# Gathers of a conv-attention kernel taken image by image, and a quarter of the third image's keys and values made inside the attention

## The chip, the cores and the metric

The kernel runs on one core of a Trainium2 chip. The metric is the device time of one execution in microseconds (us). The core has five engines that work side by side, each through its own list of instructions: PE (TensorE, matmuls and transposes), DVE (VectorE), ACT (ScalarE), POOL (GpSimd) and SP (SyncE, which here only issues DMAs). They meet at semaphores.

## The reference

The input `x` is four images of 32 x 32 positions with 384 channels, in float32. Layer 0 is a deformable attention: queries, a grouped 3 x 3 convolution that gives each query and group a sampling offset, bilinear sampling of the input there, keys and values from the samples, and an attention of 1024 queries by 1024 keys for each of 4 x 6 = 24 image-and-head units, with a position bias that is itself sampled bilinearly. Cut to what matters:

```
q = gn(x) @ w_q
o = gelu(layernorm(grouped_conv3x3(q)))
pos = tanh(o @ w_offp) * 16 + ref            # for each query and each of 6 groups
xs = bilinear_sample(gn(x), pos)
k, v = xs @ w_k, xs @ w_v
attn = softmax(q_h . k_h * scale + bilinear_sample(rpe, (ref - pos) / 2))
x = x + (attn @ v) @ w_out
```

Layer 1, a linear attention and a mixture of four experts on the result, follows. The change doesn't touch it.

## The kernel before, in words

**Stage A** makes, for all four images, what the attention needs. An image b is split into two halves f of 512 positions, and into eight blocks k of 128. The steps have one-letter names in the code:

- x and rec load an image (`x`) and write the records that are gathered later (`img`); T transposes it; S is the group norm's statistics.
- Q makes queries, C the convolution (L712, with its copies L724 and L738 on ACT), N the offsets: statistics (L761), scaling (L774 on ACT, L778 and L780 on DVE), Gelu (L782), products and sums (L788, L795), Tanh (L799), then nine small DVE operations from `pos` (L802) to the gather's indices `pidx` (L823), and after them the weights of the four corners and `widx`, the indices of the attention's windows. N comes in halves of an image; image 0's first half comes in two quarters.
- G is `fetch(b, k)` (L866): six indirect DMAs by POOL (L870), one for each group, into one of four buffers `ga`. M is `sampled(b, k)` (L880): three DVE operations (L885, L889, L890) that weight and sum the corners into `xs`.
- X transposes a sampled half (L256, copied with scale and shift by ACT, L262), K makes its keys (three blocks, `keys_of`, L269; ACT L278; stored by SP, L281), V its values (four blocks, `values_of`, L285; ACT L294; stored by SP, L298). `mm` and `tr` are the PSUM buffers that they take.

The order of these steps is not left to a scheduler at run time. `Plan.emit` (L118) simulates the stage: each step has an engine, a cost, a rank and needs, and some take and give back buffers; the step that can start first goes first, by rank where several can. The ranks are shifted by the table `SHIFT`, with an entry for each group of steps. The outcome is a fixed order of instructions on PE, ACT, DVE, POOL and SP, written out by hand. In the program's final order the attention's first window gather (POOL) and its `upper` (ACT) stand ahead of the last steps of stage A.

Image 3 is different: its samples are made in stage A, but its X, K and V are left to the attention (`if b == B - 1: continue`).

**Stage B, the attention**, runs 24 units i in six heads for each image, in four steps kp each, so 96 steps g. A step holds two blocks of 128 keys by 1024 queries. POOL gathers two windows of the bias (`fetch_windows`, L1161), which are interpolated by ACT (`upper`, L1177), DVE (`lower`, L1187) and ACT (`left`, L1195). PE adds scores and bias in PSUM (L1214, L1219) and DVE finishes them (`right`, L1245), runs the maximum (L1263), subtracts (L1304); ACT takes the exponential (L1308), PE multiplies with the values (L1322) and sums (L1331), ACT copies the result (L1347). A one-column copy on ACT, the `token` (`turn_over`, L1234), tells PE that a score buffer is free. Five steps of the loop overlap: step g runs scores of g + 1, `upper` of g + 2 and values of g - 5.

Between these, `late` is a list of pieces: for each half of image 3, two transposes, three keys and four values. `last_image(0)` puts one piece on PE in a PSUM tile `pl` at the end of an even step, unless the output projection (`project`) has blocks waiting; `last_image(1)` evacuates it by ACT and stores it by SP in the next odd step. So pieces are made at kp 0 or 2. Step 60 loads weights for what follows (`load_early`).

**Stages C and D**, layer 1, follow from about 1750 us.

Of the kernel before, what the change touches and what calls it, by code (L numbers as in the profile page):

```python
# [20 lines left out]
B, HI, WI, NC = 4, 32, 32, 384  # L21
N = HI * WI
NB = N // P
CK = NC // P
G, GC = 6, 64
# [24 lines left out]


SHIFT = {
    ("ACT", "N", 0, 2): 71.86, ("ACT", "N", 3, 4): -5.4, ("ACT", "S", 2): -1.66,
    ("ACT", "evac", 0): 9.11, ("ACT", "evac", 3): -1.37, ("DVE", "M", 0, 0): 25.81,
    ("DVE", "M", 1, 0): 43.51, ("DVE", "N", 0, 0): 2.62, ("DVE", "N", 0, 4): -14.96,
    ("DVE", "N", 1, 0): -6.58, ("DVE", "N", 1, 4): -10.24, ("DVE", "N", 3, 0): 10.74,
    ("DVE", "N12", 2, 0): 12.78, ("DVE", "N13", 0, 4): -4.3, ("DVE", "N14", 3, 4): 7.9,
    ("DVE", "S", 1): -23.97, ("DVE", "S", 2): -4.87, ("DVE", "S", 3): 21.73,
    ("PE", "C", 1, 0): -15.62, ("PE", "C", 2, 0): 257.27, ("PE", "C", 2, 1): -80.64,
    ("PE", "C", 3, 1): -31.12, ("PE", "KV", 2, 1): -162.62, ("PE", "Q", 0, 0): 127.94,  # L60
    ("PE", "Q", 0, 1): 192.74, ("PE", "Q", 1, 1): -31.15, ("PE", "Q", 2, 1): 132.86,
    ("PE", "Q", 3, 0): -20.06, ("PE", "Q", 3, 1): -65.0, ("PE", "T", 1, 0): 250.72,
    ("PE", "T", 1, 1): 49.56, ("PE", "T", 2, 0): -10.46, ("PE", "T", 2, 1): -7.45,
    ("PE", "X", 0, 0): 318.41, ("PE", "X", 0, 1): 228.46, ("PE", "sh"): 162.66,
    ("SP", "S", 1): 13.19, ("SP", "table"): -9.72, ("SP", "wv"): 63.45, ("SP", "x", 1): 6.66,
    ("SP", "x", 3): 32.23,
}


# [89 lines left out]
def body(  # L159
# [120 lines left out]
    def keys_store(kt, b, f, c):  # L280
        nc.sync.dma_start(k_d[b][c][:, f * 512 : (f + 1) * 512], kt)  # L281
# [18 lines left out]
    with tc.tile_pool(name="a_w", bufs=1) as aw, tc.tile_pool(name="a_1", bufs=1) as a1, tc.tile_pool(  # L300
# [621 lines left out]
        for b in range(B):  # L922
# [56 lines left out]
            for f in range(2):  # L979
# [21 lines left out]
                sizes = (K4 // 2, K4 // 2) if b == f == 0 else (K4,)  # L1001
                for i, n in enumerate(sizes):
                    k0, r = K4 * f + i * n, n / K4
                    o_done = i == len(sizes) - 1
                    plan.chain(
                        ("N", b, k0), offsets(b, k0, n),
                        [
                            ("DVE", 2.8 * r + 0.2, 3 + b + 0.2 * i), ("ACT", 1.6, 1), ("DVE", 1.2, 3 + b + 0.2 * i), ("ACT", 2.9 * r, 1),
                            ("DVE", 1.7 * r + 0.1, 3 + b + 0.2 * i), ("DVE", 1.7 * r + 0.1, 3 + b + 0.2 * i), ("ACT", 1.4 * r + 1.4, 1),
                            ("DVE", 1.7 * r + 0.1, 3 + b + 0.2 * i), ("DVE", 1.7 * r + 0.1, 3 + b + 0.2 * i),  # L1010
                            ("DVE", 1.7 * r + 0.1, 3 + b + 0.2 * i), ("DVE", 1.7 * r + 0.1, 3 + b + 0.2 * i), ("ACT", 1.6, 1),
                            ("DVE", 2.2, 2), ("DVE", 1.5, 2.5 + b), ("DVE", 2.8, 7 + b),
                        ],
                        {
                            0: {
                                "needs": [("C", b, f, c, 3) for c in every] + ["parts"],
                                "takes": [("mv", (b, k0))],
                            },
                            2: {"gives": [("mv", (b, k0))]},
                            7: {"takes": [("pr", (b, k0, 0)), ("off", (b, k0))]},  # L1020
                            8: {"gives": [("pr", (b, k0, 0))]},
                            9: {
                                "takes": [("pr", (b, k0, 1))], "gives": [("o", (b, f))] if o_done else [],
                                "needs": [("N", b, k0 - n, 9)] if i else [],
                            },
                            10: {"gives": [("pr", (b, k0, 1))]},
                            12: {"gives": [("off", (b, k0))], "takes": [("w", (b, k0)), ("pidx", (b, k0))]},
                            13: {"gives": [("w", (b, k0))], "takes": [("w4", (b, k0))]},
                        },
                    )  # L1030
                for k in range(4 * f, 4 * f + 4):
                    k0 = k // sizes[0] * sizes[0]
                    done = (k + 1) % sizes[0] == 0
                    step(
                        ("G", b, k), "Pool", 8.6, 1 + b + 0.01 * k, (lambda b=b, k=k: fetch(b, k)),
                        [("N", b, k0, 12), ("S", b, 16)] + [("rec", b, i) for i in range(2 * G)],
                        takes=[("ga", (b, k))], gives=[("pidx", (b, k0))] if done else [], lag=2.6,
                    )
                    step(
                        ("M", b, k), "DVE", 3.4, 2.2 + b, (lambda b=b, k=k: sampled(b, k)),  # L1040
                        [("G", b, k), ("N", b, k0, 13)] + ([("M", b, k - 1)] if k % K4 else []),
                        takes=[(f"xs{b % 2}{f}", (b, f))] if k % K4 == 0 else [],
                        gives=[("ga", (b, k))] + ([("w4", (b, k0))] if done else []),
                    )
                if b == B - 1:
                    continue
                for c in every:
                    plan.chain(
                        ("X", b, f, c), turned(b, f, c),
                        [("PE", 0.65, x_at + 10 * f - 1), ("ACT", 0.85, 2)],  # L1050
                        {
                            0: {
                                "takes": ["tr"] + ([(f"xsT{f}", (b, f))] if c == 0 else []),
                                "gives": [(f"xs{b % 2}{f}", (b, f))] if c == CK - 1 else [],
                                "needs": [("M", b, k) for k in range(4 * f, 4 * f + 4)] + ([("X", b, f, 0, 0)] if c else []),
                            },
                            1: {"gives": ["tr"]},
                        },
                    )
                for c in every:  # L1060
                    plan.chain(
                        ("K", b, f, c), keys(b, f, c),
                        [("PE", 2.8, x_at + 10 * f + (0.5, 1.5, 3.5)[c]), ("ACT", 0.75, 2), ("SP", 1.2, 5)],
                        {
                            0: {"takes": ["mm"], "needs": [("X", b, f, i, 1) for i in every] + ["wk"]},
                            1: {"takes": ["kt"], "gives": ["mm"]}, 2: {"gives": ["kt"], "lag": 2.5},
                        },
                    )
                for k4 in range(4):
# [9 lines left out]
                            2: {"gives": [(f"vt{k4 % 3}", (b, f, k4))], "lag": 2.5},  # L1079
                        },  # L1080
                    )
        plan.emit({"ACT": 4.5, "Pool": 9.0, "DVE": 1.0, "PE": 2.0, "SP": 0.5})
        by_hand.close()


# [22 lines left out]
    with tc.tile_pool(name="b_w", bufs=1) as bwp, tc.tile_pool(name="b_qkv", bufs=2) as bq, tc.tile_pool(  # L1108
# [327 lines left out]


        late = []
        for f in range(2):
            late += [("t", f, (0, 1)), ("t", f, (2,))]  # L1440
            late += [("k", f, c) for c in range(CK)] + [("v", f, k4) for k4 in range(4)]

        def last_image(part):
            if part == 0 and late and not waiting:
                what, f, at = late.pop(0)
                pl = bps.tile([P, 2, 512], F32, tag="x", name=f"pl{len(late)}")
                if what == "t":
                    for i, c in enumerate(at):
                        turn(pl[:, i, :], B - 1, f, c)
                elif what == "k":  # L1450
                    keys_of(pl[:, 0, :], f, at)
                else:
                    values_of(pl[:, 0, :], f, at)
                state["late"] = what, f, at, pl
            elif part == 1 and "late" in state:
                what, f, at, pl = state.pop("late")
                if what == "t":
                    for i, c in enumerate(at):
                        turn_copy(pl[:, i, :], B - 1, f, c)
                elif what == "k":  # L1460
                    keys_copy(bkv[:, 0:512], pl[:, 0, :], at)
                    keys_store(bkv[:, 0:512], B - 1, f, at)
                else:
                    values_copy(pl[:, 0, :], at)
                    values_store(B - 1, f, at)


        with tc.manual_schedule(
# [22 lines left out]
            for g in range(NP + 7):  # L1491
# [11 lines left out]
                else:  # L1503
                    running(g)
                    if kp == 2:
                        to_queries(i - 2, 1)
                    else:
                        project(2)
                        last_image(1)
                turn_over(g + 1)  # L1510
                values(g - 5, 1)
                if kp == 2:
# [11 lines left out]
                elif kp == 1:  # L1524
                    to_queries(i - 2, 0)
                if kp % 2 == 0:
                    last_image(0)
                    project(0)
                for e in range(2):
                    if kp:  # L1530
# [665 lines left out]
```

## Time and profile before

| what | value |
|---|---|
| time before, median of 3 runs | 2959.43 us (2949.66 to 2962.03) |
| the profiled execution | 2872.47 us, span 2870.8 us |
| its mean granted TensorE clock | 0.965 |
| busy: PE, DVE, ACT, POOL | 91%, 55%, 40%, 29% of the span |
| gathers (POOL L870) | 192, the first at 89.39 us, the last ends at 401.28 us |
| first `right` of the attention (DVE L1245) | 431.37 us |

The profiled execution is 3% shorter than the median of the runs, so durations that come from it describe an execution of 2872.47 us. In the timelines, each line gives start, duration, engine, line, operation, output and inputs; the brackets give the idle time of the engine just before and what released it. A line such as "x12" stands for twelve instructions in a row. [...]

### The profile page before, as it was taken

How to read it: one execution, taken by the hardware profiler on the slowest of the kernel's cores; microseconds unless marked ns; L12 is line 12 of the kernel's file. 1: busy time of each engine (PE TensorE's matmuls, PEld its weight loads, DVE VectorE, ACT ScalarE, POOL GpSimd, SP SyncE). 2: the span in 40 equal slices, each digit the busy share in tenths (PEclk: the TensorE clock that was granted, in tenths of full speed). 3: DMA queues.
4: the chain of work that ended last, by engine and by line, in shares of the span. 5: the costliest groups of instructions: out<-in, count | busy, mean ns of one | idle time of the engine just before them, and what ended most of it. 6: DMA issues, size and time to landing. Idle time of an engine off the chain costs nothing. (4 is left out here: it accounts for less than half of the span.)

```text
span 2870.8 us, 33282 instructions
## 1 busy us (share of the span) xinstructions
PE 2602.4 (91%) x12731; PEld 1294.0 (45%) x12731; DVE 1589.5 (55%) x2357; ACT 1147.6 (40%) x1521; POOL 824.9 (29%) x744
## 2 busy tenths in 40 slices
PE   8888757889898888888799998999999999999999
PEld 5555422323333333233356554555555555555566
DVE  2897848999999999999647766010111011011011
ACT  4565426776767767766323222111111111111121
POOL 1668852322333332332001124211112111021121
PEclk8989979999999999999899999999999999999999
DMA  7844574455555554554121311722223433374371
GB/s 193 238 148 123 167 215 139 143 153 157 152 160 171 173 161 143 146 158 126 28 99 45 125 45 57 259 104 102 102 102 108 143 137 137 120 252 171 112 266 60
DMA packets 267899, 404.77 MB, mean 141 GB/s; under 512 B 134674, under 2 KB 207634, under 8 KB 267356
## 3 DMA queue, kind: packets, MB, share of 16 engines
q1 hardware_dynamic: 214912, 230.43, 25.3%
q0 software_dynamic: 52112, 172.15, 18.5%
q8 instruction: 100, 1.64, 0.2%
q14 instruction: 59, 0.48, 0.1%
q10 hardware_dynamic: 716, 0.07, 0.0%
HBM read 345.68 MB, written 70.06 MB: 145 GB/s over the span
## 5 line engine op out<-in xcount | busy, mean ns | idle before, releaser
L2043 PE MATMUL ph<-d_xT,w 128*128 128x512 f32 (+1 forms) x1152 | 483.5, 554 | 1.2 <-ACT h L2050 1.2
L2075 PE MATMUL acc<-w,h 128*128 128x384 f32 x1392 | 480.3, 486 | 0.0
L1161 POOL DMA_INDIRECT win<-table,widx x192 | 278.8, 1452 | 647.6 <-DVE t L1187 615.6
L1214 PE MATMUL ps<-q,k 64*64 64x512 f32 x1536 | 379.4, 609 | 66.6 <-DVE S L1245 47.9
L2050 ACT ACTIVATE h<-ph,b1c 128x512 f32<-128x512 f32 (+1 forms) x192 | 124.2, 647 | 776.2 <-PE ph L2043 761.7
L1219 PE MATMUL ps<-o,ident 64*64 64x512 f32 x1536 | 377.5, 610 | 0.0
L2075 PEld LDWEIGHTS acc<-w,h 128*128 128x128 f32 x1392 | 264.1, 190 | 208.5 <-issue 73.2
L2043 PEld LDWEIGHTS ph<-d_xT,w 128*128 128x128 f32 x1152 | 216.7, 191 | 196.2 <-issue 144.5
L870 POOL DMA_INDIRECT ga<-img,pidx x192 | 237.7, 1238 | 148.6 <-DMA img<-in_x 75.6
L2105 POOL DMA_INDIRECT out<-rows,ei x67 | 67.2, 1002 | 701.2 <-DVE rows L2102 692.4
L1308 ACT ACTIVATE S<-S 128x2048 f32<-128x2048 f32 x96 | 183.4, 1910 | 194.4 <-DVE S L1304 194.4
L1187 DVE SCALAR_TENSOR_TENSOR t<-win,bw,t 128x1056 f32<-128x1056 f32 x192 | 244.6, 1315 | 17.3 <-ACT t L1177 16.1
L1245 DVE SCALAR_TENSOR_TENSOR S<-t,bw,ps 128x1024 f32<-128x1024 f32 x192 | 237.0, 1276 | 26.9 <-PE ps L1219 23.8
L1699 DVE COPY d_xT<-e_tr 128x512 f32<-128x512 f32 (+2 forms) x75 | 36.6, 512 | 385.9 <-PE e_tr L1696 385.9
L1214 PEld LDWEIGHTS ps<-q,k 64*64 64x64 f32 x1536 | 100.3, 134 | 328.2 <-issue 184.6
L2094 DVE SCALAR_TENSOR_TENSOR rows<-b2r,en,rows 128x384 f32<-128x384 f32 x67 | 41.0, 618 | 362.1 <-DMA rows<-out,ei 294.4
L1177 ACT ACTIVATE t<-win,bw 128x1056 f32<-128x1056 f32 x192 | 217.9, 1168 | 32.3 <-DMA ga<-img,pidx 27.1
L1195 ACT ACTIVATE o<-t,bw 128x1024 f32<-128x1024 f32 x192 | 212.9, 1144 | 29.4 <-DVE t L1187 23.9
L1322 PE MATMUL po<-S,v 128*64 128x512 f32 x768 | 198.1, 639 | 24.4 <-ACT av L1347 15.2
L1304 DVE TENSOR_TENSOR S<-S,pbs 128x2048 f32<-128x2048 f32 x96 | 219.0, 2283 | 2.0 <-ACT pbs L1299 2.0
L2102 DVE SCALAR_TENSOR_TENSOR rows<-acc,en,rows 128x384 f32<-128x384 f32 x67 | 41.4, 618 | 218.4 <-PE acc L2075 216.8
L1832 POOL DMA_INDIRECT tab_d<-ent,si x64 | 62.3, 974 | 246.0 <-DVE r_fl L1855 227.1
(350 smaller groups left out, 3488.7 us busy)
## 6 DMA issues: line engine op xcount, KB each, us to landing
w<-in_L_ffn_w SPq DMA_DIRECT2D x50, 2304.0 KB
img<-in_x SPq DMA_DIRECT2D x48, 256.0 KB
q<-q_d SPq DMA_DIRECT2D x48, 256.0 KB
x<-in_x SPq DMA_DIRECT2D x8, 768.0 KB
q_d<-qt SPq DMA_DIRECT2D x24, 256.0 KB
v_d<-qkvw SPq DMA_DIRECT2D x32, 192.0 KB
v<-v_d SPq DMA_DIRECT2D x24, 256.0 KB
k<-k_d SPq DMA_DIRECT2D x48, 128.0 KB
```

The source lines that it names most:

```text
L870: nc.gpsimd.indirect_dma_start(out=ga[:, g].rearrange("p s c -> p (s c)"), out_offset=None, in_=img[b][:, :], in_offset=bass.IndirectOffse ...
L1161: nc.gpsimd.indirect_dma_start(out=win, out_offset=None, in_=tables[h // 2][:, :], in_offset=bass.IndirectOffsetOnAxis(ap=widx[b][:, nb, h ...
L1177: nc.scalar.activation(t.rearrange("p y x -> p (y x)"), wins[p, e][:, : HI * WIN], AF.Copy, scale=weight(p, e, 0),)
L1187: nc.vector.scalar_tensor_tensor(tf, wins.pop((p, e))[:, WIN:], weight(p, e, 1), tf, ALU.mult, ALU.add)
L1195: nc.scalar.activation(o, ts[p, e][:, :, 0:WI], AF.Copy, scale=weight(p, e, 2))
L1214: made.append(nc.tensor.matmul(ps[HALF[1 - r], e, FULL[f]], k[HALF[r], 2 * kp + e, :], q[HALF[r], FULL[f]], start=(step == 0), stop=(step ...
L1219: made.append(nc.tensor.matmul(ps[HALF[r], d, FULL[f]], ident[HALF[r], HALF[r]], os_[p, d][HALF[r], FULL[f]], start=(step == 0), stop=(ste ...
L1245: nc.vector.scalar_tensor_tensor(st[:, e, :].rearrange("p (y x) -> p y x", x=WI), ts.pop((p, e))[:, :, 1:WIN], weight(p, e, 3), ps[:, e, : ...
L1304: nc.vector.tensor_tensor(Ss[p], Ss[p], bc(pbss[p // KP][:, :], 1, 2), ALU.add)
L1322: nc.tensor.matmul(pos[i][0][HALF[f], :], vs[i][:, 2 * kp + e, :], Ss[p][:, e, FULL[f]], start=(first and e == 0), stop=(last and e == 1),)
L2043: nc.tensor.matmul(ph if short(d) else ph[:, :n], a, m, start=(c == 0), stop=(c == CK - 1))
L2075: nc.tensor.matmul(d["acc"][0 if short(d) else s][:, :NC], h[:, s * P : (s + 1) * P], d["w2"][:, hc, :], start=(hc == 0), stop=(hc == HC - 1),
```

## The change

It has four parts.

1. A gather of image b now needs all gathers of image b - 1, and in image 2 those of the second half need those of the first. Before, the planner was free there, and gathered image 2's second half and image 3's second half first.
2. The time that a gather takes to land (2.6 us in the planner) is no longer part of G's own completion but a step L of its own on an imagined queue, on which M waits. The gathers that need earlier gathers don't wait for their landing.
3. N's ranks are made of the half's place, so that image 0's first quarter is taken ahead of its second; and the whole table `SHIFT` is another, so that the order on every engine of stage A is new. X of image 2's second half follows X of its first.
4. K and V of image 2's second half (three keys, four values) leave stage A and are the first pieces in `late`. Values now go in pairs: a piece holds two blocks, both halves of the tile `pl`, with two evacuations and two stores. The list has 19 pieces instead of 18. The work is the same in sum; `last_image` is called `last_pieces`.

In the new order of instructions ACT has all evacuations of keys and values of stage A ahead of the attention's first `upper`; before, two value copies were behind it. On PE the stage ends with the transposes of image 2's second half and with keys and values of image 1's first half. On POOL the gathers go image 0, 1, 2 in order, then image 3's second half and its first, and all windows come after them; before, one window gather stood before the last block. On DVE the last `sampled` of image 3 has the first `lower` inside it.

The diff, its table `SHIFT` cut:

```
@@ -50,20 +50,21 @@
 
 
 SHIFT = {
-    ("ACT", "N", 0, 2): 71.86, ("ACT", "N", 3, 4): -5.4, ("ACT", "S", 2): -1.66,
...
-    ("SP", "x", 3): 32.23,
+    ("ACT", "N", 1, 0): -2.56, ("ACT", "N", 1, 4): -11.36, ("ACT", "N", 3, 0): 14.8,
+    ("ACT", "evac", 0): 29.38, ("ACT", "evac", 2): 14.44, ("ACT", "evac", 3): -2.88,
...
+    ("SP", "x", 3): 26.92,
 }
 
 
@@ -1001,15 +1002,15 @@
                 sizes = (K4 // 2, K4 // 2) if b == f == 0 else (K4,)
                 for i, n in enumerate(sizes):
                     k0, r = K4 * f + i * n, n / K4
-                    o_done = i == len(sizes) - 1
+                    o_done, at = i == len(sizes) - 1, 3 + b + 2 * i - (2 if b == f == 0 else 0)
                     plan.chain(
                         ("N", b, k0), offsets(b, k0, n),
                         [
-                            ("DVE", 2.8 * r + 0.2, 3 + b + 0.2 * i), ("ACT", 1.6, 1), ("DVE", 1.2, 3 + b + 0.2 * i), ("ACT", 2.9 * r, 1),
-                            ("DVE", 1.7 * r + 0.1, 3 + b + 0.2 * i), ("DVE", 1.7 * r + 0.1, 3 + b + 0.2 * i), ("ACT", 1.4 * r + 1.4, 1),
-                            ("DVE", 1.7 * r + 0.1, 3 + b + 0.2 * i), ("DVE", 1.7 * r + 0.1, 3 + b + 0.2 * i),
-                            ("DVE", 1.7 * r + 0.1, 3 + b + 0.2 * i), ("DVE", 1.7 * r + 0.1, 3 + b + 0.2 * i), ("ACT", 1.6, 1),
-                            ("DVE", 2.2, 2), ("DVE", 1.5, 2.5 + b), ("DVE", 2.8, 7 + b),
+                            ("DVE", 2.8 * r + 0.2, at), ("ACT", 1.6, 1 + i), ("DVE", 1.2, at), ("ACT", 2.9 * r, 1 + i),
+                            ("DVE", 1.7 * r + 0.1, at), ("DVE", 1.7 * r + 0.1, at), ("ACT", 1.4 * r + 1.4, 1 + i),
+                            ("DVE", 1.7 * r + 0.1, at), ("DVE", 1.7 * r + 0.1, at),
+                            ("DVE", 1.7 * r + 0.1, at), ("DVE", 1.7 * r + 0.1, at), ("ACT", 1.6, 1 + i),
+                            ("DVE", 2.2, 2 + i), ("DVE", 1.5, 2.5 + b), ("DVE", 2.8, 7 + b),
                         ],
                         {
                             0: {
@@ -1033,12 +1034,15 @@
                     done = (k + 1) % sizes[0] == 0
                     step(
                         ("G", b, k), "Pool", 8.6, 1 + b + 0.01 * k, (lambda b=b, k=k: fetch(b, k)),
-                        [("N", b, k0, 12), ("S", b, 16)] + [("rec", b, i) for i in range(2 * G)],
-                        takes=[("ga", (b, k))], gives=[("pidx", (b, k0))] if done else [], lag=2.6,
-                    )
+                        [("N", b, k0, 12), ("S", b, 16)] + [("rec", b, i) for i in range(2 * G)]
+                        + [("G", b - 1, i) for i in range(NB) if b]
+                        + [("G", b, i) for i in range(k0) if b == B - 2],
+                        takes=[("ga", (b, k))], gives=[("pidx", (b, k0))] if done else [],
+                    )
+                    step(("L", b, k), "queue", 0.0, 0, lambda: None, [("G", b, k)], lag=2.6)
                     step(
                         ("M", b, k), "DVE", 3.4, 2.2 + b, (lambda b=b, k=k: sampled(b, k)),
-                        [("G", b, k), ("N", b, k0, 13)] + ([("M", b, k - 1)] if k % K4 else []),
+                        [("L", b, k), ("N", b, k0, 13)] + ([("M", b, k - 1)] if k % K4 else []),
                         takes=[(f"xs{b % 2}{f}", (b, f))] if k % K4 == 0 else [],
                         gives=[("ga", (b, k))] + ([("w4", (b, k0))] if done else []),
                     )
@@ -1052,11 +1056,14 @@
                             0: {
                                 "takes": ["tr"] + ([(f"xsT{f}", (b, f))] if c == 0 else []),
                                 "gives": [(f"xs{b % 2}{f}", (b, f))] if c == CK - 1 else [],
-                                "needs": [("M", b, k) for k in range(4 * f, 4 * f + 4)] + ([("X", b, f, 0, 0)] if c else []),
+                                "needs": [("M", b, k) for k in range(4 * f, 4 * f + 4)] + ([("X", b, f, 0, 0)] if c else [])
+                                + ([("X", b, 0, 2, 0)] if b == B - 2 and f else []),
                             },
                             1: {"gives": ["tr"]},
                         },
                     )
+                if (b, f) == (B - 2, 1):
+                    continue
                 for c in every:
                     plan.chain(
                         ("K", b, f, c), keys(b, f, c),
@@ -1079,7 +1086,7 @@
                             2: {"gives": [(f"vt{k4 % 3}", (b, f, k4))], "lag": 2.5},
                         },
                     )
-        plan.emit({"ACT": 4.5, "Pool": 9.0, "DVE": 1.0, "PE": 2.0, "SP": 0.5})
+        plan.emit({"ACT": 4.5, "Pool": 9.0, "DVE": 1.0, "PE": 2.0, "SP": 0.5, "queue": 0.0})
         by_hand.close()
 
 
@@ -1436,33 +1443,36 @@
 
 
         late = []
-        for f in range(2):
-            late += [("t", f, (0, 1)), ("t", f, (2,))]
-            late += [("k", f, c) for c in range(CK)] + [("v", f, k4) for k4 in range(4)]
-
-        def last_image(part):
+        for b, f in ((B - 2, 1), (B - 1, 0), (B - 1, 1)):
+            if b == B - 1:
+                late += [("t", b, f, (0, 1)), ("t", b, f, (2,))]
+            late += [("k", b, f, c) for c in range(CK)] + [("v", b, f, (k4, k4 + 1)) for k4 in (0, 2)]
+
+        def last_pieces(part):
             if part == 0 and late and not waiting:
-                what, f, at = late.pop(0)
+                what, b, f, at = late.pop(0)
                 pl = bps.tile([P, 2, 512], F32, tag="x", name=f"pl{len(late)}")
                 if what == "t":
                     for i, c in enumerate(at):
-                        turn(pl[:, i, :], B - 1, f, c)
+                        turn(pl[:, i, :], b, f, c)
                 elif what == "k":
                     keys_of(pl[:, 0, :], f, at)
                 else:
-                    values_of(pl[:, 0, :], f, at)
-                state["late"] = what, f, at, pl
+                    for i, k4 in enumerate(at):
+                        values_of(pl[:, i, :], f, k4)
+                state["late"] = what, b, f, at, pl
             elif part == 1 and "late" in state:
-                what, f, at, pl = state.pop("late")
+                what, b, f, at, pl = state.pop("late")
                 if what == "t":
                     for i, c in enumerate(at):
-                        turn_copy(pl[:, i, :], B - 1, f, c)
+                        turn_copy(pl[:, i, :], b, f, c)
                 elif what == "k":
                     keys_copy(bkv[:, 0:512], pl[:, 0, :], at)
-                    keys_store(bkv[:, 0:512], B - 1, f, at)
+                    keys_store(bkv[:, 0:512], b, f, at)
                 else:
-                    values_copy(pl[:, 0, :], at)
-                    values_store(B - 1, f, at)
+                    for i, k4 in enumerate(at):
+                        values_copy(pl[:, i, :], k4)
+                        values_store(b, f, k4)
 
 
         with tc.manual_schedule(
@@ -1506,7 +1516,7 @@
                         to_queries(i - 2, 1)
                     else:
                         project(2)
-                        last_image(1)
+                        last_pieces(1)
                 turn_over(g + 1)
                 values(g - 5, 1)
                 if kp == 2:
@@ -1524,7 +1534,7 @@
                 elif kp == 1:
                     to_queries(i - 2, 0)
                 if kp % 2 == 0:
-                    last_image(0)
+                    last_pieces(0)
                     project(0)
                 for e in range(2):
                     if kp:
```

## The prediction

> **What bounds the kernel now.** I read the page's busy shares and its 40 slices first, then the groups, then the timelines of POOL, of the last 90 us of stage A, and of two attention steps.
>
> ```profile
> PE   8888757889898888888799998999999999999999
> DVE  2897848999999999999647766010111011011011
> POOL 1668852322333332332001124211112111021121
> ```
>
> A slice is 72 us: stage A is slices 1 to 6, the attention (24 units of four steps) runs to slice 24, the rest is PE-bound and not touched. In slices 2 to 5 of stage A DVE and PE are both nearly full, but the sixth has gaps on every engine. POOL's digits understate it: between two gathers it pays 0.30 us that do not count as busy.
>
> ```profile
> 89.39 1.01 POOL L870 DMA_INDIRECT ga<-img,pidx  x1 [75.62 <-DMA img<-in_x]
> 162.86 1.29 POOL L870 DMA_INDIRECT ga<-img,pidx  x1 [0.30 <-issue]
> 179.23 0.95 POOL L870 DMA_INDIRECT ga<-img,pidx  x1 [15.08 <-DVE pidx L823]
> 392.10 0.94 POOL L1161 DMA_INDIRECT win<-table,widx  x1 [0.30 <-issue]
> 400.05 1.23 POOL L870 DMA_INDIRECT ga<-img,pidx  x1 [0.30 <-issue]
> ```
>
> This is POOL's timeline (start, duration, then the idle time ahead and its releaser). After the first gather POOL is a chain of 192 gathers with one gap, 15.08 us for image 1's indices. Image 0's 48 take 164.15 - 89.39 = 74.8 us. The other 144 and one window gather (0.94 + 0.30) take 401.28 - 179.23 = 222.05 us, so 1.534 us each. POOL sets the end of stage A: what the attention needs comes after its last gather. I call the end of that gather E; before, E = 401.28.
>
> ```profile
> 396.33 1.17 ACT L1177 ACTIVATE t<-win,bw 128x1056 f32<-128x1056 f32 x1 [27.08 <-DMA ga<-img,pidx]
> 397.42 0.84 ACT L294 COPY qkvw<-psv 128x384 f32<-128x384 f32 x2
> 397.93 6.10 PE L285 MATMUL psv<-qkvw,xT 128*128 128x384 f32 x12 [25.53 <-ACT qkvw L294]
> 409.14 9.47 PE L269 MATMUL psk<-xT,qkvw 128*128 128x512 f32 x18 [3.80 <-ACT xT L262]
> 418.44 7.90 PE L285 MATMUL psv<-qkvw,xT 128*128 128x384 f32 x24
> 426.96 0.72 PE L1214 MATMUL ps<-q,k 64*64 64x512 f32 x2 [0.61 <-ACT qkvw L294]
> ```
>
> Here is the tail. ACT stood for 27.08 us at the attention's first window operation, whose window is a gather queued in POOL at 392.10. Two value copies (L294) are behind it on ACT, so PE stood for 25.53 us; then a half-image of keys and values, 9.47 + 7.90 us, lies between E and the first scores. The first `right` (L1245) starts at 431.37, 30.1 us after E.
>
> [...]
>
> **The change, part by part.**
>
> *First gather.* Before, ACT's scaling of image 0's first half (L774) stood behind two conv copies of the second half:
>
> ```profile
> 64.55 0.84 ACT L724 ACTIVATE oT<-pcv,cols 128x256 f32<-128x256 f32 x2 [5.77 <-PE pcv L712]
> 66.61 0.96 DVE L778 TENSOR_TENSOR o<-o,lng 128x768 f32<-128x768 f32 x1 [5.95 <-ACT o L774]
> ```
>
> The new order puts those copies after the first half's scaling and both Gelus, and the conv tile that feeds the statistics about 2 us earlier (55.35 becomes 53.3). Then scaling ends near 61.2 instead of 67.8, L780 near 64, the Gelu table load (1.28) and first Gelu near 66.2. Eight L788/L795 at some 0.9 give 7.2 us, three L561 2.1, the nine small operations to `pidx` 1.9: the first gather goes at 77.5 instead of 89.39.
>
> *Gaps.* In the new DVE order `pidx` of image 0's second half stands behind `sampled(0,3)`. 24 gathers from 77.5 take 37.0 us (as from 89.39 to 126.35); landing of the last is 2.3 later (issue end to DVE start, as at 223.91 to 226.24), `sampled` 3.2 (L885, L889, L890: 1.76 + 0.96 + 0.56, slightly overlapped), two L561 1.4, the nine operations 2.2. So the 25th gather goes at 123.2, a new gap of 8.7 us, and image 0 ends at 123.2 + 37.8 = 161.0. Image 1's `pidx` again stands behind `sampled(0,7)`, then L778, L795, L780 and an L561 (5.8), then 2.2: 2.3 + 3.2 + 5.8 + 2.2 = 13.5, so image 1 starts at 174.5 (before 179.23). What waits behind these DVE waits is the next half's offsets, already counted.
>
> *Image by image.* Forcing the order adds no instruction; it decides when indices are needed. With no further gap: image 2 at 174.5 + 73.6 = 248.1, its second half at 284.9, image 3's halves at 321.7 and 358.5. Before, the four halves' indices were ready at 241.3, 290.3, 316.0 and 357.4. At that pace the second would cost 5.4 us and the others nothing. DVE's work is the same, however, and its order now serves these halves in this sequence; I take 0, with 0 and 10 as bounds. E = 174.5 + 144 x 1.534 = 395.4, **5.9 us earlier**.
>
> *Tail.* In the new order ACT has every key and value copy ahead of the first window operation, and PE has no keys or values left that wait for image 2's last gathers. 3 keys (2.66 each) and 4 values (2.02) of `(2,1)` leave, 16 us of PE. After E: window issue 1.3, landing 3.3, four windows at 1.3 spacing, L1177 1.17 for the last, token, scores, L1195 1.15: some 16.5 us to `right(0)` instead of 30.1. That is **13.6 us**, bounds 8 and 16, and the total is 19.5 us: `right(0)` at 411.9.
>
> *Attention.* The same 16 us return as pieces: 19 instead of 18, because values go in pairs. A step (from one `right` to the next) is 7.41, 9.38, 10.22, 12.16 us for kp 0 to 3; pieces sit at kp 0 and 2, and their evacuation at kp 1 and 3.
>
> ```profile
> 591.90 2.20 PE L285 MATMUL pl<-qkvw,xT 128*128 128x384 f32 x6
> 594.37 1.94 PE L1322 MATMUL po<-S,v 128*64 128x512 f32 x8 [0.27 <-ACT av L1347]
> ```
>
> A single value block fits the slack: the next values wait for ACT's `av` until 594.37 anyway. Single pieces move the interval by 0.13 (value) and 0.32 (key, 2.66 us) at kp 0, and by nearly 0 and 0.3 at kp 2. A pair is 4.04 us: PE starts the next values at 596.0, 1.6 late, and the wait for the ACT token (0.35 at 599.53) and others absorb some 0.7; ACT's two copies (0.48 each, in sequence) stand ahead of the token. I take 0.9 a pair at either place; nothing before shows a pair, so the bounds are 0 (all in slack) and 2.4 (4.04 less the 1.6 of slack). Six pairs 5.4, three more keys 0.9, eight single values gone -0.5: **5.8 us lost**, bounds 0 and 16. Their stores are the same DMAs, at other times; SP has room. POOL's window gathers of the steps don't move.
>
> *Sum.* -19.5 + 5.8 = -13.7 us on the profiled 2872.47 us (span 2870.8, some 1.7 around it). The median of the runs, 2959.43, is 3% longer than that execution; scaled, -14.1, so **2945 us**, just at the edge of what can be told. [...]
>
> **Rivals.** A measurement of this kernel can tell about 0.5%, 14.8 us, from no change.
>
> *The attention gives it back.* Pairs outlast PE's slack and most of the 16 us of moved work return, or gaps of 5 to 10 us remain at the image boundaries. For: L1214's scores wait only for DVE, and the step of 9.38 has under 2 us of PE idle. Against: keys of 2.66 us cost only 0.32. Then -4 to -10: 2949 to 2955, no change.
>
> *POOL starves (slower).* With images forced in sequence POOL can't take another image's half when indices are late, and every us lands on E. Each of the four later halves' indices stands in DVE's order among `sampled` of the image before, which waits for gathers: a loop in which DVE waits for POOL's landing and POOL for DVE, as in the 15.08 us gap. The price is a landing, a `sampled`, the remaining offsets: some 12 us a boundary. Slower by 14.8 needs 13.7 + 14.8 = 29 us, so three of the four boundaries; with three it is 36 - 14 = +22, 2981. For: slack of 0.3 us before (290.3 against 290.6). Against: image 1 to 3's `pidx` stand well ahead in the new DVE order, except the second half of image 2, behind `sampled(2,2)`.
>
> *The order does little.* Image 1 was already after image 0, so forcing acts on the halves of images 2 and 3 only, and the first gather may come no earlier (other work on ACT). Then only the tail remains, -13.6 + 5.8 = -8: 2951.
>
> *More.* The pair hides wholly and the chain is as worked out: -20 to -25, 2934 to 2939.
>
> **How the numbers follow.** Forecast 0.40 (2938 to 2950, 0.22 of it beyond 0.5%), more 0.22, attention gives back 0.13, little done 0.08, starving 0.17. Faster 0.44, same 0.37, slower 0.19 (starving, and a little of the giving back with a gap beside it). The range 2925 to 2976: the low end is 28 us of stage A with nothing lost, and some 5 of spread between medians; the high end takes in most of a starved POOL. The likeliest case alone, 2938 to 2950.
>
> **What would show it.** First gather near 77.5; a gap near 9 us before the 25th; one near 13.5 before image 1; none over 3 us later; E near 395; no 25 us wait at L294; keys and values of `(2,1)` under the tile `pl`; `right(0)` near 412; steps with pairs longer by about a microsecond. Wrong if POOL shows gaps on `pidx` after 175, or if the attention's span from `right(0)` to its end grows by over 12 us.

## The result, and the profile after

The runs give 2915.02 us for the changed kernel (2913.84 to 2921.35) against 2960.65 us before (2949.66 to 2962.03): a ratio of 0.9858, interval 0.983 to 0.9886, so 45 us by the medians. The forecast was 2945 us with a range down to 2925. The sign was right; three times the forecast gain came, and the time lies below the range.

The profile after is of an execution of 2916.14 us (span 2914.4). That is longer than the 2872.47 us of the profile before, though the kernel is faster: the first profile of before was not like its timed executions, and a second one of the same kernel took 2967.88 us (`b_again` below). The page's slices, of 73 us here:

```profile
PE   8679957888898988889799997999999999999999
DVE  3668867999999999999647665101001101011011
POOL 1528873232333323233000223322111112121121
```

In the second and third slices of stage A PE and DVE are emptier than before, and POOL is nearly idle in the third, so something holds all three. Next the timeline of POOL after, as before: start, duration, idle time ahead with its releaser.

```profile
78.38 1.02 POOL L871 DMA_INDIRECT ga<-img,pidx  x1 [64.34 <-DMA x<-in_x]
128.75 0.94 POOL L871 DMA_INDIRECT ga<-img,pidx  x1 [13.62 <-DVE w L828]
210.56 0.94 POOL L871 DMA_INDIRECT ga<-img,pidx  x1 [52.13 <-DVE w L828]
431.06 0.94 POOL L871 DMA_INDIRECT ga<-img,pidx  x1 [0.30 <-issue]
```

The first gather is where it was forecast, and so is the place of both gaps. But the second is 52 us instead of 13.5, and E is 432 instead of 395. The timeline of PE says why:

```profile
131.62 1.52 PE L713 MATMUL pcv<-qpad,wc 64*64 64x256 f32 x22
...
141.33 0.58 PE L713 MATMUL pcv<-qpad,wc 64*64 64x256 f32 x1 [1.53 <-issue]
144.13 0.58 PE L713 MATMUL pcv<-qpad,wc 64*64 64x256 f32 x1 [2.23 <-issue]
146.23 0.58 PE L713 MATMUL pcv<-qpad,wc 64*64 64x256 f32 x1 [1.51 <-issue]
149.03 0.58 PE L713 MATMUL pcv<-qpad,wc 64*64 64x256 f32 x1 [2.22 <-issue]
...
162.33 0.58 PE L713 MATMUL pcv<-qpad,wc 64*64 64x256 f32 x1 [0.82 <-issue]
```

A conv tile of 72 matmuls, which takes 4.12 us at 124.86, takes over 32 us here. Between single matmuls PE stands for 0.8 to 2.9 us and waits for nothing that the profile shows ("issue"). I call this a **creep**. ACT's copies stand behind that tile, DVE behind ACT, and POOL behind DVE's indices. ACT's timeline shows the first link:

```profile
171.18 0.87 ACT L725 ACTIVATE oT<-pcv,cols 128x256 f32<-128x256 f32 x2 [20.16 <-PE pcv L713]
```

The tail, in the timelines of ACT and DVE, is as it was forecast: the copies end before the windows come, and `right` (now L1252) starts 19.3 us after E.

```profile
396.51 4.99 ACT L491 COPY sh<-pt_sh 128x480 f32<-128x480 f32 x6
437.89 1.17 ACT L1184 ACTIVATE t<-win,bw 128x1056 f32<-128x1056 f32 x1 [36.39 <-DMA win<-table,widx]
451.30 2.47 DVE L1252 SCALAR_TENSOR_TENSOR S<-t,bw,ps 128x1024 f32<-128x1024 f32 x2 [2.38 <-PE ps L1226]
```

A pair in the attention, on PE's timeline, where single blocks took 2.20 us and the values then waited for ACT's `av`:

```profile
535.37 4.14 PE L286 MATMUL pl<-qkvw,xT 128*128 128x384 f32 x12
539.44 1.94 PE L1329 MATMUL po<-S,v 128*64 128x512 f32 x8
```

The values wait for nothing now: PE itself is late, as was expected of a pair.

### The profile page after: what moved, and what is told of

Read it like the earlier page. It is cut to its first block, busy times and chain, and to the rows that moved or that the text cites. A ratio compares the mean times of both kernels' runs of the same rounds, so it can differ in the third digit from the quotient of the medians.

```text
span 2914.4 us, 33271 instructions
## 1 busy us (share of the span) xinstructions
PE 2620.1 (90%) x12731; PEld 1295.6 (44%) x12731; DVE 1589.4 (55%) x2357; ACT 1149.0 (39%) x1522; POOL 817.4 (28%) x744
## 5 line engine op out<-in xcount | busy, mean ns | idle before, releaser
L871 POOL DMA_INDIRECT ga<-img,pidx x192 | 230.3, 1199 | 187.7 <-DVE w L828 65.7
L1252 DVE SCALAR_TENSOR_TENSOR S<-t,bw,ps 128x1024 f32<-128x1024 f32 x192 | 236.9, 1275 | 21.0 <-PE ps L1226 18.0
L1329 PE MATMUL po<-S,v 128*64 128x512 f32 x768 | 197.7, 638 | 23.8 <-ACT av L1354 13.6
L713 PE MATMUL pcv<-qpad,wc 64*64 64x256 f32 x1728 | 121.4, 396 | 27.3 <-issue 26.6
```

The source lines that it names most:

```text
L871: nc.gpsimd.indirect_dma_start(out=ga[:, g].rearrange("p s c -> p (s c)"), out_offset=None, in_=img[b][:, :], in_offset=bass.IndirectOffse ...
L1252: nc.vector.scalar_tensor_tensor(st[:, e, :].rearrange("p (y x) -> p y x", x=WI), ts.pop((p, e))[:, :, 1:WIN], weight(p, e, 3), ps[:, e, : ...
L1329: nc.tensor.matmul(pos[i][0][HALF[f], :], vs[i][:, 2 * kp + e, :], Ss[p][:, e, FULL[f]], start=(first and e == 0), stop=(last and e == 1),)
```

## The experiments

Sessions differ. In two, before takes 2880 us at the median and the profiles show no long creep; in the session of the result and four more, it takes 2959 to 2970 us, with creeps. None was mixed: no execution of before took over 2891 us in the first kind or under 2949 in the second. The two quiet sessions ran on chips 8 and 9, the four later ones with creep on chips 5, 10 (twice) and 14, so it may go with the chip; no chip was seen in both kinds, and those of the result and of the first profile aren't known. Ratios are always to before in the same session. The table compares profiles, in us:

| | before, first profile | before again | after | after again | after, third |
|---|---|---|---|---|---|
| long creep | no | yes | yes | yes | no |
| first gather | 89.39 | 86.86 | 78.38 | 76.43 | 76.43 |
| POOL's gaps over 1 us, sum | 15.1 | 96.0 | 65.8 | 89.5 | 25.6 |
| the rest of E, gathers | 296.8 | 288.1 | 287.9 | 277.6 | 292.7 |
| E | 401.28 | 470.92 | 432.0 | 443.51 | 394.77 |
| first `right` | 431.4 | 505.0 | 451.3 | 464.2 | 412.5 |
| last `right` starts | 1375.7 | 1450.7 | 1403.9 | 1417.0 | 1363.0 |
| span | 2870.8 | 2966.2 | 2914.4 | 2935.4 | 2863.9 |

### Both kernels again

`b_again` and `a_again` are the two kernels with no edit.

> The kernel before, unchanged, run again with a profile. Theory 1[...]: the profiled execution of before was one with hardly any of them (no gap of PE with 'issue' over 3 us in stage A), while the timed ones, 78 to 90 us longer, have them; a profile of an execution at 2950 to 2962 then shows POOL gaps on pidx that add up to 50 us or more over the 15 of the first profile, with PE's conv matmuls (L712) creeping one by one in the same stretch. Theory 2 (nothing special in a place): the 3% are spread over all stages in proportion, and stage A ends within 15 us of 401 + 30. Ratio to before 1.00 either way.

> The kernel after, unchanged. Theory 1: the creep of PE at 132 to 163 us that its profile shows belongs to its ordinary executions too: again a POOL gap near 50 us before image 1, E near 430, total near 2915, ratio near 0.985. Theory 2: the creep was an accident of one execution, the gap is some 13 us now, E near 395 and the execution near 2880.

Measured: before again 0.9993 (0.9979 to 1.0006), after again 0.9876 (0.9852 to 0.9901). POOL's timeline of `b_again`, with its gaps:

```profile
153.94 1.14 POOL L870 DMA_INDIRECT ga<-img,pidx  x1 [13.65 <-DVE d L889]
166.25 1.14 POOL L870 DMA_INDIRECT ga<-img,pidx  x1 [4.91 <-DVE d L889]
211.88 0.95 POOL L870 DMA_INDIRECT ga<-img,pidx  x1 [38.23 <-DVE pidx L823]
271.44 1.14 POOL L870 DMA_INDIRECT ga<-img,pidx  x1 [19.50 <-DVE d L889]
358.68 0.94 POOL L870 DMA_INDIRECT ga<-img,pidx  x1 [19.68 <-DVE w L827]
```

That makes 96.0 us of gaps instead of 15.1. PE's timeline has creeps in conv tiles (L712) at 124 to 143, 225 to 254 and, shorter, 326 to 337 us; each of the larger gaps follows one. The gaps and creeps are those that theory 1 expected; what PE waits for in them isn't shown. Between these two profiles the change takes 27.4 us from E (470.92 to 443.51; 10.4 by the first gather, 6.5 by fewer gaps, 10.5 by shorter gathers), 13.4 from the way from E to the first `right` (34.1 to 20.7), gives back 7.1 in the attention (945.7 to 952.8) and 2.9 later: -30.8 in all. In `a_again` the creep at 141 to 168 us remains, and no long one after it.

> The kernel after once more, since the executions of before in one session take 2970 us and in another 2880. If PE's instruction stream creeps here (before near 2970): POOL gaps of 14 to 28 and some 52 us, E 430 to 445, ratio 0.985 to 0.988. If not (before near 2880): first gather near 77, gaps near 11.7 and 13, E near 394, right(0) near 412, attention 6 us longer, ratio 0.995 (14 us less).

`a_third`, again the kernel after, came in a session without creep: 0.9964 (0.9953 to 0.9975), 10 us less than before where 14 were expected. Its timelines of POOL and DVE:

```profile
124.59 0.94 POOL L871 DMA_INDIRECT ga<-img,pidx  x1 [11.65 <-DVE w L828]
174.33 0.94 POOL L871 DMA_INDIRECT ga<-img,pidx  x1 [13.96 <-DVE w L828]
```

```profile
412.54 2.47 DVE L1252 SCALAR_TENSOR_TENSOR S<-t,bw,ps 128x1024 f32<-128x1024 f32 x2 [0.64 <-PE ps L1226]
```

The prediction had 8.7 and 13.5 for these gaps and 411.9 for this `right`.

### What PE's creep hangs on: the records or the gathers

`before_bigrec` and `after_bigrec` copy the records in long runs, so other data of x is gathered. Two small copies for each image, for rows that this leaves out, are cut here.

```
-                image(b)[g, 1 - e : 1 - e + HI, 1 : WP - 1, e, :],
-                x[b, :, :, g * GC : (g + 1) * GC],
+                img[b].rearrange("(g y x) c -> g y (x c)", g=G, y=HI + 1)[
+                    g, y : y + n, 2 * GC : (WP - 1) * 2 * GC
+                ],
+                x[b].rearrange("h w c -> (h w c)")[g * 65536 : g * 65536 + n * 4096]
+                .rearrange("(y c) -> y c", y=n),
...
```

> The kernel before, with the same number of record DMAs (48) of about the same size, but each copies runs of 16 KB instead of runs of 256 bytes, so what is gathered is other data of x. Theory 1a (the creep of PE's instructions comes from the many small packets of the records): the creep at 124 to 143 us goes, POOL's gaps of 13.7, 4.9 and 38.2 us become about 15 in all, E falls from 471 by 30 to 45 us and the time by as much (0.985 to 0.99). Theory 1b (the gathers' own packets do it): the creeps stay, and only the 16 DMA engines are freer: within 5 us (0.998 to 1.002). The creep at 226 to 254, when no records are moved, stays under both.

> The kernel after with the same edit of the records (other data of x is gathered). Theory 1a: the one creep that it has, at 134 to 168 us, goes, the gaps of 14 to 28 and 52 us become the 8.7 and 13.5 of the prediction, E near 395, time near 2890 (0.975 of before). Theory 1b: E stays near 432 to 443, time near 2925.

Both came in a session without creep: 0.9995 (0.9985 to 1.0005) and 0.9968 (0.9954 to 0.9982), so they decide nothing on it; repeated in the other such session as `before_bigrec2` and `after_bigrec2`, 0.9988 (0.9979 to 0.9996) and 0.9968 (0.9957 to 0.998). With creep, at last:

> The kernel before with records copied in runs of 16 KB (other data of x is gathered). Without creep (before near 2880): 0.999 again. With creep (before near 2970): theory 1a,[...] 0.985 to 0.99 and no creep near 124 to 143 us; theory 1b,[...] 0.998 to 1.002 with the creep still there.

> The kernel after with the same edit of the records (other data of x is gathered). Without creep 0.997 again. With creep: theory 1a 0.97 to 0.975, no creep at 134 to 168 us and E near 395; theory 1b 0.985 to 0.988 and E near 440.

1.0004 (0.9991 to 1.0016) and 0.9876 (0.9855 to 0.9897), with the creeps at 123 to 143 and 224 to 254, and at 133 to 160. Between 60 and 175 us the hardware queue moves 7097 packets in `before_bigrec3` where `b_again` has 38861. So theory 1a falls: the records' small packets are not the cause. That leaves the gathers, and the DMA view of `b_again` fits them. Each line is a queue with its packets, MB and share of the DMA engines. From 240 to 250 us, within the second creep, the gathers (the software queue) are all that flows:

```profile
q0 software_dynamic: 384, 1.05, 34.3%
```

They aren't enough for a creep: in the first profile of before, from 130 to 140 us, they flow as well, and PE runs the conv tiles there, of 72 matmuls, in 4.12 and 4.47 us.

```profile
q1 hardware_dynamic: 5321, 1.80, 71.8%
q0 software_dynamic: 302, 0.83, 26.6%
q8 instruction: 1, 0.02, 0.6%
```

The packets of queue 8, which the DMA view labels `instruction`, show no fixed relation to a creep. In `after` none of them starts from 132 to 158 us, within the creep, and one comes between 158 and 166, where it ends. But over the span queue 8 has one packet to about 255 of PE's matmuls and weight loads (100 packets, 25462 of them), so that none falls among PE's 33 matmuls there says little. In `b_again` one does come from 224 to 240 us, within the second creep, with the gathers flowing; PE creeps on to 253.93, and from 240 to 256 none comes. The DMA view from 224 to 240 us, and PE's timeline:

```profile
q0 software_dynamic: 532, 1.45, 31.6%
q1 hardware_dynamic: 144, 0.26, 4.3%
q8 instruction: 1, 0.02, 0.4%
```

```profile
253.93 7.21 PE L712 MATMUL pcv<-qpad,wc 64*64 64x256 f32 x75 [1.50 <-issue]
```

What the profiles do show: each of their fourteen long creeps (18 us or more, in the nine runs without an added pause that have them) ends 2.0 to 5.3 us after the last gather ahead of a gap of POOL. Which of the two ends the other, added idle work on POOL tells (`before_hold`, two such pauses; `after_hold` has the first alone):

```
+            if (b, k) in ((0, 5), (1, 2)):
+                hold = a3.tile([P, 320], F32, tag="hold", bufs=1, name=f"hold{b}")
+                for _ in range(36):
+                    nc.gpsimd.memset(hold, 0.0)
             ga = a3.tile([P, G, 2, 2 * GC], F32, tag="ga", bufs=4, name=f"ga{b}_{k}")
```

> The kernel before, with the same 11 us of idle work on POOL between blocks 4 and 5 of image 0 and again between blocks 1 and 2 of image 1. With creep, theory 1b: the creeps at 124 to 143 and 225 to 254 end some 5 and 10 us earlier, and the time is 0 to 20 us less (0.993 to 1.0) in spite of 22 us of added work. Rival: +5 to +22 us (1.002 to 1.007). Without creep: +10 to +22 us (1.003 to 1.008).

> The kernel after, with some 11 us of idle work put on POOL (36 memsets of a scratch tile) between the gathers of image 0's blocks 4 and 5, nothing left out. Where PE creeps (before near 2960 to 2970): theory 1b, [...]has the creep that began near 132 end near 145 instead of 160 to 168, so PE's conv, then the indices of image 1 come some 15 to 20 us earlier, and a kernel with idle work added is faster than after by 5 to 20 us (0.979 to 0.985 of before). Rival: the creep has a length of its own and its end stops the gathers rather than the other way: E and the time rise by 0 to 11 us (0.987 to 0.991). Without creep (before near 2880): image 0 ends 11 us later, of which the wait for image 1's indices of 13 us hides little: +4 to +11 us on after (0.998 to 1.0).

With creep in the session, `before_hold` takes 0.9941 (0.9924 to 0.9958) of before: 30.4 us of pauses are added to the engine that sets E, and it is faster by 17 us, within the forecast of theory 1b. Its timelines of POOL and PE:

```profile
134.14 15.20 POOL L871 MEMSET hold<- 128x320 f32 x36
194.00 0.94 POOL L874 DMA_INDIRECT ga<-img,pidx  x1 [15.08 <-DVE pidx L823]
```

```profile
134.01 1.01 PE L712 MATMUL pcv<-qpad,wc 64*64 64x256 f32 x2 [0.82 <-issue]
135.41 2.24 PE L712 MATMUL pcv<-qpad,wc 64*64 64x256 f32 x10 [0.39 <-issue]
...
140.30 4.12 PE L712 MATMUL pcv<-qpad,wc 64*64 64x256 f32 x72
```

The creep ends 1.3 us into the pause, and the next whole conv tile takes 4.12 us; the creep near 225 us doesn't come, the gaps are gone but for the 15.08 us of the first profile, and E is 433.73. `after_hold` takes 0.9854 (0.9833 to 0.9876). Its timelines of POOL and PE:

```profile
139.32 15.17 POOL L872 MEMSET hold<- 128x320 f32 x36
```

```profile
140.65 9.72 PE L713 MATMUL pcv<-qpad,wc 64*64 64x256 f32 x115 [1.29 <-issue]
```

Its creep, of three single matmuls where after has twelve, also ends 1.3 us into the pause, so a creep has no fixed length. The gap before image 1 is 12.93 us, E 417.48. So in these runs the gathers keep a long creep going, not the other way round; whether their packets or POOL's work of issuing them is what holds PE, and by what path, wasn't separated. Against 0.9858 and 0.9876 for after in other sessions the time is no clear gain, and it falls short of the 0.979 to 0.985 that theory 1b forecast: the pause costs about what it brings.

> The kernel after with a third of the pause of after_hold (12 memsets, some 5 us by the 15.2 us that 36 took), at the same place, nothing left out. With creep (before near 2960): if PE needs only a few us without gathers[...], the creep near 132 to 140 ends within the pause, E comes 10 us earlier than with the long pause (near 407) and the ratio is 0.980 to 0.984. If 5 us are too short, the creep goes on to 160 and the ratio is 0.986 to 0.989. Without creep (before near 2880): +2 to +5 us on after (0.997 to 0.998).

`after_hold5` (`range(12)`, a pause of 5.02 us) takes 0.9863 (0.9845 to 0.9882), not the 0.980 to 0.984 forecast for this case: PE's creep does end in the pause, 0.8 us after its start, but the gap before image 1 is still 43.43 us, for now ACT waits:

```profile
178.13 0.84 ACT L725 ACTIVATE oT<-pcv,cols 128x256 f32<-128x256 f32 x2 [32.89 <-remote]
```

The conv tile in question was done by 158; the 32.89 us have no releaser in the profile. The wait ends 3.4 us after POOL's last gather of image 0, as the creeps of PE do, but no run shows what held ACT. No version tried is clearly better than the changed kernel.

### The move alone, the pairs alone, the order alone

`move_only` is before with the last seven K and V steps of its stage A (there image 2's first half) put into the attention, `pairs_only` before with image 3's values in pairs:

```
+                if (b, f) == (B - 2, 0):
+                    continue
...
+        for b, f in ((B - 2, 0), (B - 1, 0), (B - 1, 1)):
```

> The kernel before with its own order of stage A, but K and V of a half of image 2 (there the first half, whose seven steps stand last in that order) made in the attention, values in pairs. Gathers unchanged. If the tail is worth what was predicted: right(0) comes 13 to 17 us after where keys and values stood, attention loses 6 to 8, so -6 to -10 us against before (0.997 to 0.998). If most of the 45 us came with the move (PE tail): -30 us or more (0.99). If the gain is in the order of stage A alone: within 5 us of before (0.998 to 1.002).

> The kernel before with image 3's values in pairs, nothing else: four pairs instead of eight single pieces, list of 14 pieces. Forecast by the prediction's prices: 4 x 0.9 - 0.5 = +3 us (1.001). If a pair is hidden wholly: 0. If pairs pay all of their excess over the slack: 4 x 2.4 - 0.5 = +9 us (1.003).

With creep: 0.9987 (0.9977 to 0.9998) and 1.001 (0.9999 to 1.0021). In `move_only` the way from E to the first `right` is 20.4 us where `b_again` has 34.1: 13.7 us, the tail as it was priced; the attention is 3.4 us longer; E came 6.8 us later in that one profile. The time falls by less than the 6 to 10 us expected. The pairs cost about 3 us, as forecast, at the edge of what can be told. A repeat of the move,

> The kernel before with its own order and the seven last K and V steps of stage A (image 2's first half) made in the attention. Without creep: E unchanged near 402, right(0) 13 to 14 us earlier, attention 5 to 6 us longer, so -7 to -9 us (0.997). With creep 0.9987 again.

again with creep, gave 0.9981 (0.9972 to 0.9989), 6 us, with an attention 7.0 us longer. So the move, with the pairs, is worth 4 to 6 us of the 45 in the old order.

`before_order` is before with its own table, and only the conditions for G added:

```
+                        + [("G", b - 1, i) for i in range(NB) if b]
+                        + [("G", b, i) for i in range(k0) if b == B - 2],
```

> The kernel before with its own table of shifts, and only the condition added that gathers go image by image, and in image 2 by halves. If forcing the order is what gains, E comes 15 to 27 us earlier and the time is 0.99 of before. If the condition by itself does nothing good, because the gain is in the new order of the other engines, POOL waits at the image boundaries for indices in the old order of DVE: E the same or later by up to 20 us, 0.999 to 1.007.

1.0055 (1.0038 to 1.0072), in a session without creep: slower. POOL's timeline has a new gap of 28.67 us ahead of image 2's first gather, and E is 426.4. The conditions by themselves make a worse kernel. Under the new table they don't bind: without them the planner writes the same order on every engine. So, by subtraction, most of the gain comes with the rest of the new order (table, ranks, the step L); no run has these parts one by one.

`after_stage` is after with `continue` for image 2's second half taken out, so that its K and V are made in stage A.

> The kernel after, with its order of stage A, but K and V of image 2's second half made in stage A again (image 3's values still in pairs). Prediction's prices: 16 us of PE come back to stage A, the attention gets back three keys and two pairs, 2.7 us. If E is set by POOL and its waits alone and PE has room: E unchanged, time 0 to 3 us less than after (0.986 to 0.987 of before). If PE's 16 us lie on the way to the indices or to the first scores: 5 to 16 us more than after (0.99 to 0.993).

> The kernel after, with K and V of image 2's second half made in stage A (image 3's values in pairs). Without creep 1.001 again: E near 394 as in after, but the first scores wait for the k that SP loads behind the values' stores. With creep: that wait of some 22 us is there too, so 0.993 to 0.996 where after has 0.986 to 0.988; if creep hides it, 0.986 to 0.99.

Without creep 1.0012 (1.0004 to 1.0021), which the first expectation, stated for a session with creep, didn't cover; with creep 0.9933 (0.9912 to 0.9953), as the second had it. E is 394.36 without creep, as in `a_third` (394.77): PE's 16 us are not on the way to E. PE's timeline has the price elsewhere:

```profile
426.29 3.01 PE L1219 MATMUL ps<-q,k 64*64 64x512 f32 x3 [52.46 <-DMA k<-k_d]
```

The first scores wait for keys, whose load SP issues only at 420.37 us, after the late values' stores (the last at 400 to 402); in `a_third` they were at hand at 393. So in the new order the move is worth 0.5% (0.9964 against 1.0012, in two sessions), in the old order 0.2%: in the new one it also takes those stores out of the way of the first keys.

## Why the prediction was right and wrong

- **First gather** 77.5: 76.4 to 78.4 in the three profiles of the changed kernel. Right.
- **Gaps** 8.7 and 13.5: 11.65 and 13.96 without creep. The places are right and no gap came at the later halves, as chosen. The first is 3 us longer: DVE was still at sums of this half's offsets until 117.3 us, which the forecast held for done, and the parts that it names add up to 9.1, not 8.7.
- **E** 395.4: 394.77 without creep. That close a hit is in part luck: 3.4 us more of gaps, made up by a first gather 1.1 us earlier and gathers 3.0 us faster in sum.
- **Tail** 13.6: 30.1 to 17.8 us without creep (12.3), 34.1 to 20.7 with it (13.4). Right.
- **Attention** +5.8: +6.2 without creep (944.3 to 950.5), +7.1 with it. A pair takes 4.14 us on PE and makes its step about 1.3 us longer at kp 0 (10.69 against 9.38), more than the 0.9 taken and inside its bounds.
- **Sum**: on the kind of execution that the first profile showed, -13.7 was forecast and -10 measured (0.9964). The layers behind the attention were 5.8 us longer there (1495.1 to 1500.9), which the sum had not; by `before_bigrec` and `after_bigrec` it is 2.2 (1498.5 to 1500.7). The attention's last `right` starts at 1375.7 us, in slice 20 of the first profile, so these layers begin there and not at slice 24 or 1750 us.
- **The step that failed** is "The median of the runs, 2959.43, is 3% longer than that execution; scaled, -14.1". It takes the 3% as spread evenly, so that the gain grows by 3% too. They are not. Of the 95 us between the two profiles of before, 69.6 lie ahead of E (80.9 more of POOL's gaps, behind a creeping PE, less 11.3 of an earlier first gather and faster gathers), 20 in the layers behind the attention (1495.1 to 1515.5), and 5 between. The forecast took a gain off an execution without those gaps: it put 15.1 us of gaps in the old order and 22.2 in the new one, 7.1 more. In executions like the timed ones the old order pays 96.0 and the new one 66 to 90, so the gaps bring 6 to 30 us instead, and E comes 27 to 39 us earlier (`b_again` against the two profiles of after), not 5.9. Of the 27.4 between the two profiles of one session, 10.5 are shorter gathers, where 1.1 was forecast; why they are shorter stays open.
- **Luck**: of the parts of that 27.4, only the first gather (10.4 us, 11.9 forecast) came as forecast. That the gaps helped the new order rather than the old one, and so the size of the gain, is luck.
- **Starving** named POOL's waits for late indices, but as a loop at the boundaries of images and for the new order alone. The runs show the waits in both orders, behind PE's creep, and more of them in the old one.

Three things stay open. Why some sessions creep and others don't: the programs are the same, and the chip is only a suspect. By what path gathers slow PE. And why the new order has one long creep where the old one has two and a short one: that was not isolated.

## What to carry to other kernels

Before a sum is made on a profile, compare its time with the runs': where it is 3% off, find the stage in which the 3% lie, or take another profile, since a fix to that stage has another price. Here PE stood for "issue" up to 2.9 us at a time between matmuls of one tile, with no wait in the profile; what flows beside such a stretch is in the DMA view, and a pause in that flow tells whether it plays a part. The view alone doesn't: here it showed the records', the gathers' and queue 8's packets beside creeps, and the pauses in the gathers ended four of them within 1.3 us. With creep in the session, the order in which a long run of gathers has two pauses beat the same order without them (`before_hold`, 0.9941).

## What the runs showed of the hardware that was not expected

PE's matmuls, for which the profile shows no wait on POOL here, creep while gathers flow, and their single steps end 0.7 to 1.3 us after an added pause begins (four pauses in three runs). The matmuls then run on in long rows: 115 in 9.72 us in `after_hold` (85 ns each), 57 ns each in the tile of 72 in 4.12 us. The creep comes in beats: matmuls start at 141.33, 144.13, 146.23 and 149.03 us in after, steps of 2.80, 2.10 and 2.80, all multiples of 0.70. One such stretch cost PE over 32 us for one tile, and a kernel of 2880 us takes 2959 to 2970 in sessions with creeps.
